# Four layers of a graph network on one core: where the mixing's weighing products stand, and how many passes stand between the steps of its chunks

## The chip, the cores and the metric

The kernel runs on one core of one Trainium2 chip. The time is device microseconds of one execution; before the change it is 1750.03 us, the median of three runs (1749.34 to 1750.75).

## What is computed

Four graph layers run one after the other over x (8 batches, 2048 nodes, 64 features) and a dense adjacency matrix of 2048 x 2048. Each ends as `x = layernorm(x + layer(x))`. The change lies in layers 0 and 1:

```
# layer 0, its end: industry = (adj / deg) @ (x @ W_ind), g = sum over hyperedges
pair = stack([industry, g])
s = tanh(pair @ fcW + fcb) @ av          # two scores per node
out = softmax(s over the two) weighs industry and g
x = layernorm(x + out)
# layer 1
deg = sum(adj + I); dinv = deg ** -0.5
x = layernorm(x + (dinv * (adj + I) * dinv) @ x @ W.T)
# layer 2 begins with softmax(relu(E @ E.T)) of the node embeddings E
```

A softmax over two scores is a sigmoid of their difference, so the kernel forms `g - 1`, `industry` and weighs their difference by `0.5 * (1 + tanh(0.5 * (s1 - s2)))`.

## The kernel before

**Tiling.** Two batches make a pair of 128 features; there are four pairs (NP = 4). The 2048 nodes are 16 tiles of 128 (t) or 4 chunks of 512 (c, NCH = 4). The transposed adjacency stays in SBUF. A product with it is made of **passes**: one pass is one matmul of 128x512 (line 172, the helper `mm`), with a 128x128 block of the left operand as weights and a 512 column piece of the adjacency. The left operand is split into a high and a low part (`v0h`, `v0l` to `v3h`, `v3l`, one pair of tiles for each chunk of nodes), so a pair needs 2 column groups x 16 tiles x 2 parts x 2 columns = 128 passes.

**The filler.** The passes do not stand in loops of their own. Generators yield after each pass, and `fill(n)` (line 420) draws n of them between other work, so that PE has passes to do while DVE, ACT and POOL work at the rest. `products` (line 342) gives layer 0's adjacency products and the degrees, 576 passes in all; `layer1` (line 1012) follows with 128 passes for each pair. When the part that a pass of layer 1 needs has not been made yet, `layer1` yields `"wait"`: that fill issues nothing and only counts a tick. Each pass counts a tick too (`tick`, line 321), and `after(n, f)` and `later(n, f)` run f so many ticks later. That is how work on DVE, ACT and POOL is put in its place; most of it is pinned in the written order (`pin`, line 838), and each engine takes its instructions in the order in which they stand.

**The mixing (end of layer 0).** 16 steps (4 pairs x 4 chunks). For chunk i:

- `mix_load` (line 871) fetches the stored product u0 and the inverse degrees; `mix_ind` (879) makes industry from it: products `pi`, then a multiplication on DVE (885). `mix_g` (887) fetches g (`gn`), transposes it on PE (`pg`) and copies it with -1 on ACT (899).
- `mix_scores` (906): four products `pf` (two batches of industry, two of g), each with a tanh on ACT (916); 5 ticks later the two differences on DVE (921); at once industry minus g on POOL (923); 8 ticks later `r + gn` on POOL (926).
- `mix_weigh` (928): two products `pd` of the differences with av, tanh on ACT (`th`, 935), and 4 ticks later the weighed difference on DVE (937).
- `mix_end` (940): transposes of it (`pt`), then, by ticks, the addition to r (957), the layer norm (853 to 865: sums on DVE, square on ACT, power on POOL, scaling on DVE) and `end` (947): r is stored to HBM (948), the load of x for chunk i + 2 is issued (305), and `l1_parts` is called for it where it is due.

The products of all these (`pi`, `pg`, `pf`, `pd`, `pt`, and layer 1's `po`) rotate through four PSUM banks (tag "mm").

**The hand-over to layer 1.** `l1_parts(p, c)` (line 963) loads the stored chunk again (`y`, 969), scales it by dinv on POOL 16 ticks later (972), and 6 ticks after that splits it: the high part on ACT (167), the low part on DVE (168). Passes of pair p then read it: chunk q of the pair's nodes is first read 16 q passes into its 128. `l1_end` (984) closes a column group with eight matmul instructions `po`, a row sum on DVE and POOL (991, 992) and a layer norm.

**E.** When all 16 chunks are stored, the pools of the mixing are closed, the memory is given to `xn`, and the embeddings are loaded into a part of it (1098). `make_el` (1105) splits them chunk by chunk and makes the bias product `pb`; `load_xn` (1005) fetches the first three pairs' results once `room` is set. What is left of the filler follows, and then layer 2's `apt_tile` (1144) and products `ua`.

DMAs are issued in order from SP's queue (loads and stores of the mixing), from ACT's (`load_xn`) and from POOL's.

Of the kernel before, what the change touches and what calls it, by code (L numbers as in the profile page):

```python
# [56 lines left out]
def tile_gnn_fast(  # L57
# [32 lines left out]
    NCH = N // C  # L90
# [8 lines left out]
    def cols(c, n=C):  # L99
        return slice(c * n, (c + 1) * n)  # L100
# [70 lines left out]
    def mm(*args, **kw):  # L171
        tc.keep_in_program_order(nc.tensor.matmul(*args, **kw))  # L172

    def transpose(dst, src):
        tc.keep_in_program_order(nc.tensor.transpose(dst, src, ident))  # L175
# [141 lines left out]
    def after(n, f, *more):  # L317

        soon.append([n, lambda: (f(), after(*more) if more else None)])

    def tick():
        for e in pending + soon:
            e[0] -= 1
        while pending and pending[0][0] <= 0:
            pending.pop(0)[1]()
        for e in [e for e in soon if e[0] <= 0]:
            soon.remove(e)
            e[1]()
# [91 lines left out]
    def fill(n):  # L420
        for _ in range(n):
            if next(filler, None) == "wait":
                tick()

    def first_parts(c, where):
        where.add(c)
        if c in mixed and c in free:
            l1_parts(0, c)
# [402 lines left out]
    def wide(c):  # L831
        return slice(c * JT, (c + 1) * JT)
# [7 lines left out]
    def normalized(pool, r, dst, centred, then):  # L840

        groups = 2 * JT
        r, dst = grouped(r), grouped(dst)
        wide_r = [P, groups, F]
        var, vare, rstd, mean = (
            pool.tile([P, groups], F32, tag=f"ln_{n}", name=f"ln_{n}", bufs=2) for n in "verm"
        )
        xc = pool.tile(wide_r, F32, tag="ln_c", name="ln_c", bufs=1)
        squares, src = (xc, r) if centred else (r, xc)

        def square():
            if not centred:
                pin(nc.vector.tensor_reduce(mean, r, AX.X, ALU.add))
                pin(nc.vector.scalar_tensor_tensor(
                    xc, mean[:, :, None].to_broadcast(wide_r), -1.0 / F, r, op0=ALU.mult, op1=ALU.add
                ))
            pin(nc.scalar.activation(squares, src, AF.Square))

        def power():
            pin(nc.vector.tensor_reduce(var, squares, AX.X, ALU.add))  # L860
            pin(nc.vector.tensor_scalar(vare, var, 1.0 / F, EPS, op0=ALU.mult, op1=ALU.add))
            pin(nc.gpsimd.tensor_tensor(rstd, vare, neg_half[:, :groups], ALU.pow))

        def scale():
            pin(nc.vector.tensor_tensor(dst, src, rstd[:, :, None].to_broadcast(wide_r), ALU.mult))
            then()

        return square, 5, power, 9, scale
    steps = NP * NCH

    def mix_load(i):
        if i < steps:
            p, c = divmod(i, NCH)
            uts[i] = mp0.tile([P, C], F32, tag="ut0", name="ut0", bufs=2)
            nc.sync.dma_start(uts[i], u0_hbm[p][:, cols(c)])
            invs[i] = mp0.tile([P, C], F32, tag="inv0", name="inv0", bufs=2)
            nc.sync.dma_start(invs[i], inv_hbm[:, cols(c)])

    def mix_ind(i):

        pi = lps.tile([P, C], F32, tag="mm", name="pi", bufs=4)
        mm(pi, lhsT=bd_ind, rhs=uts.pop(i), start=True, stop=True)
        inds[i] = mp.tile([P, C], F32, tag="ind", name="ind", bufs=3)
        inv = invs.pop(i)
        after(3, lambda: pin(nc.vector.tensor_tensor(inds[i], pi, inv, ALU.mult)))

    def mix_g(i):

        p, c = divmod(i, NCH)
        gn = mp.tile([P, JT, P], F32, tag="gn", name="gn", bufs=2)  # L890
        nc.sync.dma_start(
            gn, gs_hbm.rearrange("(p t) f -> p t f", t=NT)[:, wide(c), p * P:(p + 1) * P]
        )
        gns[i] = gn
        pg = lps.tile([P, C], F32, tag="mm", name="pg", bufs=4)
        for j in range(JT):
            transpose(pg[:, cols(j, P)], gn[:, j, :])
        gts[i] = mp.tile([P, C], F32, tag="gt", name="gt", bufs=2)
        pin(nc.scalar.activation(gts[i], pg, AF.Identity, bias=-1.0))

    def mix_x(i):
        if i < steps:
            rs[i] = mp.tile([P, JT, P], F32, tag="r", name="r", bufs=2)
            load_x(rs[i], *divmod(i, NCH))

    def mix_scores(i):

        t1 = []
        for src in (inds[i], gts[i]):
            for b in range(2):  # L910

                s = slice(b * F, (b + 1) * F)
                pf = lps.tile([P, C], F32, tag="mm", name="pf", bufs=4)
                mm(pf, lhsT=fc2[s, :], rhs=src[s, :], start=True, stop=True)
                t1.append(mp.tile([P, C], F32, tag="t1", name="t1", bufs=4))
                pin(nc.scalar.activation(t1[-1], pf, AF.Tanh, bias=fcb_col))
        tts[i] = t1[0:2]

        def differences():
            for b in range(2):  # L920
                pin(nc.vector.tensor_tensor(t1[b], t1[b], t1[2 + b], ALU.subtract))

        pin(nc.gpsimd.tensor_tensor(inds[i], inds[i], gts[i], ALU.subtract))
        after(5, differences)
        r, gn = rs[i], gns.pop(i)
        after(8, lambda: pin(nc.gpsimd.tensor_tensor(r, r, gn, ALU.add)))

    def mix_weigh(i):

        pd = lps.tile([P, C], F32, tag="mm", name="pd", bufs=4)  # L930
        for b in range(2):

            mm(pd[b * F:(b + 1) * F, :], lhsT=av2, rhs=tts[i][b], start=True, stop=True)
        th = mp.tile([P, C], F32, tag="th", name="th", bufs=1)
        pin(nc.scalar.activation(th, pd, AF.Tanh, scale=0.5))
        after(4, lambda: pin(
            nc.vector.scalar_tensor_tensor(inds[i], th, 1.0, inds[i], op0=ALU.add, op1=ALU.mult)
        ))

    def mix_end(i):  # L940
        p, c = divmod(i, NCH)
        r = rs.pop(i)
        pt = lps.tile([P, C], F32, tag="mm", name="pt", bufs=4)
        for j in range(JT):
            transpose(pt[:, cols(j, P)], inds[i][:, cols(j, P)])

        def end():
            nc.sync.dma_start(x1_hbm[p][:, wide(c), :], r)
            mix_x(i + 2)
            stored.add((p, c))  # L950
            if p == 0:
                first_parts(c, mixed)
            elif (p, c) in due:
                l1_parts(p, c)

        def add_up():
            pin(nc.vector.scalar_tensor_tensor(
                r, pt.rearrange("p (t f) -> p t f", f=P), 0.5, r, op0=ALU.mult, op1=ALU.add
            ))

        after(3, add_up, 0, *normalized(mp, r, r, False, end))

    def l1_parts(p, c):

        if (p, c) not in stored:
            due.add((p, c))
            return
        y = staged("y")
        nc.sync.dma_start(y, x1_hbm[p][:, wide(c), :])

        def scale():
            pin(nc.gpsimd.tensor_tensor(y, y, dinv[:, wide(c), None].to_broadcast([P, JT, P]), ALU.mult))

        def cast():
            part[p, c] = split(va, y, f"v{c}", 1, [P, JT, P], pin=True)

        after(16, scale, 6, cast)
# [27 lines left out]
    def load_xn():  # L1005

        for p in range(NP - 1):
            if room and done[p] == NCH:
                done[p] = 0
                nc.scalar.dma_start(xn[p], x2_hbm[p][:])  # L1010
# [42 lines left out]
    mix_x(1)  # L1053
    fill(4)
    for i in range(steps + 1):
        k = 9 if i > NCH else 8
        if i < steps:
            mix_scores(i)
            fill(k)
        if i > 0:  # L1060
            mix_end(i - 1)
            fill(k)
        if i + 1 < steps:
            mix_load(i + 2)
            mix_ind(i + 1)
            mix_g(i + 1)
            fill(k)
        if i < steps:
            mix_weigh(i)
            fill(k)  # L1070
    while len(stored) < steps:
        fill(1)
# [43 lines left out]
        nc.scalar.copy(bias, pb)  # L1116
        nc.sync.dma_start(bias_hbm[:, wide(c), :], bias)

    fill(32)
    for c in range(NCH):  # L1120
        make_el(c)
        fill(16)
        if c == 1:

            room.append(True)
            load_xn()
# [474 lines left out]
    for u in range(2, UNITS):  # L1601
        c, k = divmod(u, 2)
# [1002 lines left out]
```

## Time and profile before

| what | value |
| --- | --- |
| median of three runs | 1750.03 us (1749.34 to 1750.75) |
| the profiled execution | 1747.23 us |
| its span, first to last instruction | 1745.0 us |
| granted PE clock, mean | 0.981 |
| PE busy | 1662.8 us, 95% of the span |
| DVE / ACT / POOL busy | 48% / 34% / 33% |
| mixing, its first scores to its last transposes | 241.5 to 463 us |
| E, its first bias product | 484.12 us |
| first product of layer 2 (`ua`) | 517.01 us |

All times of the trace are microseconds from the start of the span, and one execution was profiled. A row of the timeline has the start, the duration, the engine, the line of the code, the operation, the tile written and those read, the size, and how often; what stands in brackets is idle time of that engine ahead of it and what ended it. Matmuls overlap, so the time that one costs is read from the starts of those that follow, not from its duration. A matmul of f32 operands is two instructions in the trace.

### The profile page before, as it was taken

What the parts mean: (1) busy time and instruction counts of PE and PEld (TensorE: products, weight loads), DVE (VectorE), ACT (ScalarE), POOL (GpSimd) and SP (SyncE); (2) the same over time, 40 slices, a digit from 0 to 9 for tenths busy, and PEclk for the clock granted to TensorE, in tenths of its full rate; (3) what the DMA queues carried; (4) which work ended last, traced back from release to release, by engine and by line L of the source; (5) the groups of instructions that cost most, each with busy time, mean ns of one, the idle gap of its engine ahead of it and who ended that gap; (6) DMA issues with size and microseconds to landing.
All of it is one profiled execution on the core that took longest, in us unless ns stands there. A gap on an engine that the chain in (4) does not pass through costs nothing. (4 is left out here: it accounts for less than half of the span.)

```text
span 1745.0 us, 27987 instructions
## 1 busy us (share of the span) xinstructions
PE 1662.8 (95%) x11196; PEld 1214.8 (70%) x11196; DVE 832.9 (48%) x1547; ACT 588.9 (34%) x1031; POOL 573.6 (33%) x515
## 2 busy tenths in 40 slices
PE   6888899999989999999999989999989999999996
PEld 4666666666664444468788878888768877878775
DVE  7679945678642221210137147777623433433332
ACT  1345533434321212112213257878512222222221
POOL 4578845556534443422023001222310200202001
PEclk9899999999999999999999989999989999999998
DMA  9743344444340000017344547585571121211111
GB/s 334 253 158 124 103 131 140 151 140 145 97 141 6 30 19 12 24 66 292 111 140 130 137 105 157 133 171 131 150 273 43 49 61 43 61 47 42 57 43 39
DMA packets 171180, 195.83 MB, mean 112 GB/s; under 512 B 71536, under 2 KB 116336, under 8 KB 169760
## 3 DMA queue, kind: packets, MB, share of 16 engines
q1 hardware_dynamic: 160096, 154.54, 30.0%
q0 software_dynamic: 8544, 30.68, 5.3%
q10 hardware_dynamic: 2400, 8.72, 1.4%
q8 instruction: 90, 1.47, 0.4%
q14 instruction: 50, 0.41, 0.1%
HBM read 126.72 MB, written 67.17 MB: 111 GB/s over the span
## 5 line engine op out<-in xcount | busy, mean ns | idle before, releaser
L172 PE MATMUL ua<-pt,xn 128*128 128x512 f32 x512 | 230.2, 592 | 1.4 <-DVE pt L1150 1.4
L172 PEld LDWEIGHTS ua<-pt,xn 128*128 128x128 f32 x512 | 96.9, 190 | 111.1 <-issue 104.0
L1502 DVE COPY w_half<-pw 128x512 f32<-128x512 f32 x160 | 109.7, 705 | 91.2 <-PE pw L172 90.6
L1498 ACT COPY w_half<-pw 128x1024 f32<-128x1024 f32 x128 | 129.8, 1014 | 51.4 <-PE pw L172 51.4
L172 PE MATMUL py<-w_half,xg 128*32 128x128 f32 x4096 | 142.6, 280 | 1.2 <-issue 1.2
L172 PE MATMUL u<-adj,v0h 128*128 128x512 f32 x384 | 134.0, 426 | 1.1 <-ACT h L1800 1.1
L172 PE MATMUL u<-adj_more,v2h 128*128 128x512 f32 x384 | 126.5, 408 | 0.0
L172 PEld LDWEIGHTS py<-w_half,xg 128*32 128x32 f32 x4096 | 111.6, 138 | 18.9 <-issue 2.1
L172 PE MATMUL u<-adj,v0l 128*128 128x512 f32 x384 | 124.6, 402 | 0.0
L172 PE MATMUL u<-adj_more,v2l 128*128 128x512 f32 x384 | 124.2, 400 | 0.0
L172 PE MATMUL pw<-est,wst 64*128 64x256 f32 x1024 | 111.2, 322 | 4.9 <-ACT w_half L1498 2.7
L1156 POOL TENSOR_TENSOR acc<-acc,pt 128x512 f32<-128x512 f32 x60 | 76.5, 1274 | 104.3 <-DVE pt L1150 103.6
L172 PEld LDWEIGHTS pw<-est,wst 64*128 64x128 f32 x1024 | 84.5, 189 | 27.6 <-ACT w_half L1498 20.0
L1150 DVE TENSOR_SCALAR pt<-pt 128x512 f32<-128x512 f32 x64 | 29.6, 462 | 153.0 <-ACT pt L1149 152.8
L1709 ACT CAST ar<-fcav 128x512 fp32r<-128x512 f32 x64 | 39.5, 618 | 166.8 <-DMA fcav<-in_adj_t 165.9
L172 PE MATMUL u<-adj_more,v3l 128*128 128x512 f32 x288 | 94.2, 403 | 0.0
L172 PE MATMUL u<-adj,v1h 128*128 128x512 f32 x288 | 93.7, 403 | 0.0
L1149 ACT ACTIVATE pt<-s 128x512 f32<-128x512 f32 x64 | 38.0, 598 | 164.8 <-PE s L172 164.8
L172 PE MATMUL u<-adj_more,v3h 128*128 128x512 f32 x288 | 93.6, 403 | 0.0
L1710 DVE SCALAR_TENSOR_TENSOR ar<-fcav,ar 128x512 f32<-128x512 f32 x64 | 44.7, 698 | 100.9 <-ACT ar L1709 100.9
L172 PE MATMUL u<-adj,v1l 128*128 128x512 f32 x288 | 92.0, 397 | 0.0
L1681 POOL TENSOR_TENSOR x<-x,rows 128x512 f32<-128x512 f32 x16 | 22.7, 1439 | 210.8 <-PE pt L175 129.3
(406 smaller groups left out, 3282.6 us busy)
## 6 DMA issues: line engine op xcount, KB each, us to landing
fcav<-in_adj_t SPq DMA_DIRECT2D x64, 256.0 KB, 2.9
u_hbm<-ut SPq DMA_DIRECT2D x48, 256.0 KB, 2.8
xg<-u_hbm SPq DMA_DIRECT2D x24, 512.0 KB, 8.5
adj<-in_adj_t POOLq DMA_DIRECT2D x16, 512.0 KB, 7.7
adj_more<-in_adj_t POOLq DMA_DIRECT2D x16, 512.0 KB, 7.7
adj_hbm<-adj_more SPq DMA_DIRECT2D x16, 512.0 KB, 5.5
x_hbm<-r SPq DMA_DIRECT2D x28, 256.0 KB, 2.7
hs_hbm<-st ACTq DMA_DIRECT2D x8, 584.0 KB
```

What stands on the lines that cost most here:

```text
L172: tc.keep_in_program_order(nc.tensor.matmul(*args, **kw))
L1149: nc.scalar.activation(pt, s, AF.Exp)
L1150: nc.vector.tensor_scalar(pt, pt, 1.0, None, op0=ALU.max)
L1156: nc.gpsimd.tensor_tensor(accs[c], accs[c], pt, ALU.add)
L1498: pin(nc.scalar.copy(dst, pw.rearrange("p j o n -> p n (j o)")))
L1502: pin(copy(dst[:, :, 2 * j:2 * j + 2], bank.rearrange("p o n -> p n o")))
L1681: nc.gpsimd.tensor_tensor(xs, xs, b2.to_broadcast([P, JT, P]), ALU.add)
L1709: nc.scalar.copy(ar, seen_a)
L1710: nc.vector.scalar_tensor_tensor(ar.bitcast(F32), seen_a, 1.0, ar.bitcast(F32), op0=ALU.mult, op1=ALU.not_equal, accum_out=left[:, t, k:k ...
```

## The change

In `mix_scores` the addition `r + gn` is taken out and becomes a function of its own, `mix_sum`, called behind the loads of the next chunk. In the loop of the steps `mix_weigh(i - 1)` now stands directly ahead of `mix_scores(i)`; before, it was the last thing in its own step, with passes behind it. `mix_end(i - 1)` moves from behind the scores to the end of step i. A step has three gaps of 11 passes (12 from step 5 on) in place of four of 8 (9). In the last round, which has no scores, 24 passes stand between the weighing and the transposes. Ahead of E `fill(56)` replaces `fill(32)`, between E's chunks `fill(12)` replaces `fill(16)`, and `room` is set behind E's first chunk in place of its second.

```diff
@@ mix_scores
         pin(nc.gpsimd.tensor_tensor(inds[i], inds[i], gts[i], ALU.subtract))
         after(5, differences)
+
+    def mix_sum(i):
         r, gn = rs[i], gns.pop(i)
         after(8, lambda: pin(nc.gpsimd.tensor_tensor(r, r, gn, ALU.add)))
@@ the steps
     for i in range(steps + 1):
-        k = 9 if i > NCH else 8
+        k = 12 if i > NCH else 11
+        if i > 0:
+            mix_weigh(i - 1)
         if i < steps:
             mix_scores(i)
-            fill(k)
-        if i > 0:
-            mix_end(i - 1)
             fill(k)
         if i + 1 < steps:
             mix_load(i + 2)
             mix_ind(i + 1)
             mix_g(i + 1)
+        if i < steps:
+            mix_sum(i)
             fill(k)
-        if i < steps:
-            mix_weigh(i)
+        if i == steps:
+            fill(2 * k)
+        if i > 0:
+            mix_end(i - 1)
             fill(k)
@@ E
-    fill(32)
+    fill(56)
     for c in range(NCH):
         make_el(c)
-        fill(16)
-        if c == 1:
+        fill(12)
+        if c == 0:
             room.append(True)
             load_xn()
```

## The prediction, on record before the changed kernel ran

> **What bounds the kernel now.** I read the forty slices first: they tell which engine is never idle, and where even that one is.
>
> ```profile
> PE   6888899999989999999999989999989999999996
> PEclk9899999999999999999999989999989999999998
> ```
>
> TensorE (PE) is at nine tenths nearly everywhere. Of the stretch that the change touches (slices 6 to 12, 230 to 515 us) slice 11 alone is at 8, with a lower clock beside it. Then busy time by stretch (PE, weight loads, DVE, ACT, POOL, PE clock, DMA share, GB/s):
>
> ```profile
> 250.00:300.00 50.00, 50.00 (x218) 31.63 (x216) 27.99 (x39) 19.83 (x34) 23.59 (x22) 1.00 0.38 127
> 400.00:458.00 58.00, 58.00 (x264) 37.93 (x263) 44.38 (x64) 23.17 (x41) 37.74 (x26) 1.00 0.36 124
> 458.00:490.00 32.00, 23.98 (x95) 19.31 (x94) 20.80 (x36) 8.01 (x15) 15.05 (x11) 0.79 0.53 170
> ```
>
> Inside the mixing PE has no idle time to win. The loss sits in 32 us at its end. PE's timeline there:
>
> ```profile
> 455.37 0.63 PE L172 MATMUL u<-adj_more,v2l 128*128 128x512 f32 x2
> 455.93 1.08 PE L172 MATMUL pd<-t,fcav 128*64 128x512 f32 x4
> 456.94 0.73 PE L172 MATMUL u<-adj_more,v2h 128*128 128x512 f32 x2
> ...
> 458.91 0.40 PE L172 MATMUL u<-adj_more,v3h 128*128 128x512 f32 x1
> 462.91 1.11 PE L175 MATMUL pt<-ident,ind 128*128 128x128 f32 x4 [3.60 <-DVE ind L937]
> ...
> 479.30 0.40 PE L172 MATMUL u<-adj_more,v2l 128*128 128x512 f32 x1
> 484.12 1.93 PE L172 MATMUL pb<-bp,xn 16*128 16x64 f32 x8 [4.42 <-issue]
> ```
>
> The reader is to see two holes: the last chunk's transposes (pt) wait for its weighed difference, and E's first product (pb) waits, as the ACT row at 483.94 shows, for the embedding that the DMA brings. Behind each, for about 5 us, a pair of passes takes 0.85 us instead of 0.467 (starts 464.25, 465.10, 465.95).
>
> Last, what chunk 15 has to do between its pt and the first pass that needs it (v3h and v3l of pair 3), from the timeline of all engines:
>
> ```profile
> 465.84 0.68 DVE L957 SCALAR_TENSOR_TENSOR r<-pt,r 128x512 f32<-128x512 f32 x1
> 470.93 1.64 POOL L862 TENSOR_TENSOR ln_r<-ln_e,neg_half 128x8 f32<-128x8 f32 x1 [5.56 <-DVE ln_e L861]
> 474.14 0.32 SPq L948 DMA_DIRECT2D x_hbm<-r  x1
> 476.95 0.32 SPq L969 DMA_DIRECT2D y<-x_hbm  x1
> 479.91 1.09 POOL L972 TENSOR_TENSOR y<-y,dinv 128x512 f32<-128x512 f32 x1 [0.84 <-DMA y<-x_hbm]
> 481.03 0.62 ACT L167 CAST v3h<-y 128x512 fp32r<-128x512 f32 x1 [1.29 <-POOL y L972]
> 481.69 0.69 DVE L168 TENSOR_TENSOR v3l<-y,v3h 128x512 fp32r<-128x512 f32 x1 [1.58 <-ACT v3h L167]
> ```
>
> From pt (462.91) to v3h (481.65) are 18.7 us, 7.5 of them behind the store. Now they hide behind passes that need other chunks.
>
> **Passes as a clock.** I number the 1088 passes: 576 of the products, then 128 for each pair. 406 precede the first scores in both programs. A pass costs 0.2335 us (pairs start 0.467 apart). Pair 3 reads chunk 2's part from pass 992 and chunk 3's from 1008; pair 2 reads its chunk 3 from 880. Counting the fills: before, 24 in step 0, 32 in steps 1 to 4, 36 in 5 to 14, so chunk 15's scores stand at 918, its weighing at 936, its pt at 945. After, 22, then 33, then 36: weighing at 956, pt at 980. So pt and pass 1008 are 28 passes apart, where they were 63. In the changed program twelve of the 56 fills ahead of E find no part and issue nothing. This is the change's price.
>
> **What goes.** (a) The wait ahead of the last pt: from 458.91 to 469.10 stand 14 passes and one pt. At full speed: 14 x 0.2335 + 0.45 (pt with the slower pass behind it) = 3.7; it took 10.2. Gone: 6.5, of it 3.8 idle and 2.7 slow clock. 24 passes (5.6 us) now cover a wait of 3.8. (b) The wait ahead of pb: from 479.30 to 489.65 stand 10 passes and a pb (1.2): 3.55 of 10.35. Gone: 6.8, since 34 passes now stand between chunk 15's first use and E. (c) At the start the second pg waited 0.68 for its load (L891); it comes three passes later: 0.7. (d) Weighing and scores change the product's shape: pairs 0.467 apart become 0.56 ahead of pd and 0.57 behind it, about 0.09 and 0.10, and as much around pf. Standing together they have one return to passes less. The step from pd to pf is not in the trace; it costs between nothing and as much as both. So 0 to 0.19 in each of 15 steps; I take half, 1.5.
>
> The Trainium skill ("TensorEngine Tiling (Array Packing)", Key Properties) says that a change of tiling mode, not of tile alone, drains the engine. By it the step from pd (128x64) to pf (64x128) is such a change, one of four goes, and the sum gets 1.5 of the 2.9; no row here shows that step alone. Sum of what goes: 15.5.
>
> **What comes.** (e) Chunk 15 at pass 1008. PE arrives 0.45 + 28 x 0.2335 = 7.0 after pt's start. How late is the part? Least: chunk 13 ran undisturbed,
>
> ```profile
> 438.70 0.69 DVE L957 SCALAR_TENSOR_TENSOR r<-pt,r 128x512 f32<-128x512 f32 x1 [0.43 <-PE pt L175]
> ...
> 444.19 0.69 DVE L865 TENSOR_TENSOR r<-ln_c,ln_r 128x512 f32<-128x512 f32 x1
> ```
>
> with pt at 438.07, so 6.8 to the end of its normalization; plus 7.5 from store to v3h: 14.3. Chunk 15's own in the trace: 18.7. Most: in the changed order DVE has the low part of chunk 14 (v2l, L168) directly behind chunk 15's add, ahead of its mean. That part waits for its own y, whose buffer a pair-2 row sum (L992) frees; and POOL has two other powers (1.65 each) ahead of chunk 15's. Taking chunk 14's pt 11.9 earlier (36 passes, a pd 1.2, two po of 0.9, a pt), with the rows above I get up to 22. I take 19.5, near the row and above it for these queues: 12.5 idle. A stall this long is followed by the slow clock; both holes above lost 2.2 to 2.7 there, I take 2.4. Together 14.9 (9.7 to 17.4). Any wait of PE at 992 for chunk 14 lies inside, since chunk 15's chain does not wait for PE.
>
> (f) Chunk 11 at pass 880. Before, pt at 408.71, v3h at 427.32 (18.6 later), first used at 433.39: 6.1 to spare. After, the two are 44 passes apart instead of 61, with a pt, two po, a pd and pf (3.2), a pi with pg (1.3) and a pt between: 10.3 + 7.2 = 17.5. So 1.1 late with the same chain. Longer: the next scores now follow within 12 passes, their differences (L921) precede chunk 11's last scaling on DVE, and two of the four "mm" banks that pf rotates through belong to po just issued: up to 5. Shorter: none. I take 3.0 (0 to 5, and 2.4 more if PE cools). The trace has waits of 1.73 and 1.43 with no slow pairs behind them and of 3.60 with; 3 lies between.
>
> The Trainium skill ("TensorE: Matmul & The Clock Gate", What's actually happening) puts the limit at an idle window of about 3.4 us; by it a wait of 3.0 cools nothing, and the sum stands without those 2.4.
>
> **Costed at nothing.** mix_sum's add moves behind the next chunk's loads in POOL's and SP's order: gn's buffer comes free a step (15.2 us from pt to pt) before its transposes, its load lands in 2.9; if not, PE waits as at the start, 1.7. In the moved weighing the fourth pf takes pd's bank and waits for th (0.60 on ACT), behind three pf of 0.48; without that cover 0.6 a step. The x2 loads (L1010) are opened at E's first chunk: some 80 passes, 18 us, cover them; uncovered, the first ua would wait. No passes are left behind E's last chunk, where 29 were: the squares of the embedding now stand behind four pt on DVE, and four rounds of ua (3.67 us each) cover their load (3.7) and 1.2 of work.
>
> **Sum.** -15.5 + 14.9 + 3.0 = +2.4 us. The profiled execution took 1747.23 (span 1745.0 and 2.2 around it) and would take 1749.6; the runs shown have a median of 1750.03, so I state 1752.4.
>
> **Rivals.** 1: the parts come early. If the queues do not hold chunk 15 up, (e) is 9.7 and (f) 1.1: -4.7, 1745.3, faster. For it: chunk 13 did run so; against: v2l stands in its way. With (f) at 3.0 it decides at 17.1 us from pt to v3h. 2: chunk 11 comes in time: -0.6, 1749.4. For it: 6.1 to spare now; against: 17 passes fewer. 3: both come late and PE cools twice: 17.4 + 7.4 - 15.5 = +9.3, 1759.3. For it: queues in order, where one late load delays the next chunk; against: pair 1's last part is 60 passes from its pt (692 to 752), so nothing is late to begin with. That the change only moves the hole from pt and pb to the parts is the forecast itself.
>
> **Chances.** Forecast 0.46, rival 1 0.24, rival 2 0.14, rival 3 0.16. A measurement of this kernel tells about 0.2%, 3.5 us. The forecast, 2.4, is close to that line: 0.24 same, 0.22 slower. Rival 1: 0.22 faster, 0.02 same; rival 2: 0.02 faster, 0.10 same, 0.02 slower; rival 3: slower. Faster 0.24, same 0.36, slower 0.40. The extremes, -7.2 (all low ends) and +10.8, each need every bound at once; 1744 to 1759 leaves out the outer fifth.
>
> **What would show it.** Ahead of the last pt and of pb no wait; one hole of 10 to 14 us at the first v3h behind them, released by ACT v3h, with slow pairs behind; some 3 us at pair 2's v3h. Wrong if v3h comes under 17 us from pt, if PE waits inside the steps (pf on th or po), or if pg waits for gn in many steps.

## The result, and the profile after

The changed kernel takes 1767.57 us in the median of five runs (1763.14 to 1772.47), the kernel before 1750.72 in five runs beside it (1749.34 to 1751.01). The ratio is 1.0104, 95% interval 1.0091 to 1.0116: the change makes the kernel 1.0% slower, and the time lies above the predicted range. The profiled execution took 1763.14 us, with a span of 1761.3.

The forty slices, to be laid beside those of before:

```profile
PE   6888899989969999999999999999989999999996
PEclk9899999999989999999999989999999999999998
```

The twelfth digit, the 8 of before (480 to 523 us), has become a 6 (484 to 528), its clock has an 8 that the row of before does not show, and the ninth digit (352 to 396 us) has gone from 9 to 8. So the loss lies in the stretch that the prediction looked at, but not in one place of it only. From the first `pg` (238.45 us) to the first `ua` (536.26) the changed kernel takes 297.8 us, the kernel before 277.0 (240.01 to 517.01). These 20.8 us are more than the difference of the two spans, 16.3: outside of this stretch the profiled execution of the changed kernel happened to be 4.5 us quicker.

PE's waits between 235 and 545 us of the changed kernel (total, times, longest):

```profile
PE u L172 <- ACT v3h L167: 11.5, 1, 11.5
PE pf L172 <- ACT th L937: 4.9, 3, 3.9
...
PE pf L172 <- DVE r L993: 3.3, 2, 2.4
PE po L172 <- ACT ut L1037: 2.7, 3, 1.0
```

The first row was forecast. The waits of `pf` were not: they lie inside the steps, between the weighing and the scores that now stand behind it, and the prediction had named just these as what would show it wrong. (In the changed kernel and those made from it the lines from 926 on stand two or more later: `th` is line 937, the row sum of `po` 993. Kernels made from the one before keep its lines.) The wait of `pb`, and that of the last `pt`, are gone.

**The forecast hole.** Chunk 15 in the timeline of all engines, from its transposes to the pass that needs it:

```profile
485.35 0.60 PE L175 MATMUL pt<-ident,ind 128*128 128x128 f32 x4
487.46 0.68 DVE L959 SCALAR_TENSOR_TENSOR r<-pt,r 128x512 f32<-128x512 f32 x1
491.58 0.67 DVE L853 TENSOR_REDUCE ln_m<-r 128x8 f32<-128x512 f32 x1
498.00 0.32 SPq L950 DMA_DIRECT2D x_hbm<-r  x1
...
506.12 0.62 ACT L167 CAST v3h<-y 128x512 fp32r<-128x512 f32 x1 [12.40 <-POOL y L974]
506.79 1.22 PE L172 MATMUL u<-adj_more,v3h 128*128 128x512 f32 x2 [11.55 <-ACT v3h L167]
```

`pt` no longer waits, but from `pt` to the first pass with v3h are 21.4 us, and PE has only 28 passes to put there.

**The hole that was not forecast.** PE, POOL and ACT around the scores at 374 us:

```profile
372.08 1.28 POOL L928 TENSOR_TENSOR r<-r,gn 128x512 f32<-128x512 f32 x1 [1.46 <-DMA r<-in_x_n]
372.98 1.08 PE L172 MATMUL pd<-t,fcav 128*64 128x512 f32 x4
...
374.94 1.04 POOL L974 TENSOR_TENSOR y<-y,dinv 128x512 f32<-128x512 f32 x1
374.95 1.02 PE L172 MATMUL pf<-gt,fcav 64*128 64x512 f32 x2
376.01 0.62 ACT L167 CAST v3h<-y 128x512 fp32r<-128x512 f32 x1 [4.73 <-POOL y L974]
...
379.25 0.58 ACT L937 ACTIVATE th<-pd 128x512 f32<-128x512 f32 x1
379.88 1.23 PE L172 MATMUL pf<-gt,fcav 64*128 64x512 f32 x2 [3.91 <-ACT th L937]
```

Read it from the bottom. The fourth `pf` takes `pd`'s PSUM bank and so waits for `th`, the tanh that reads `pd`. `th` itself needs 0.58 us and could have run at 374; but ACT takes its instructions in order, and ahead of `th` stands the split of (pair 1, chunk 3), which waited 4.73 us for POOL's `y`, and behind that a square (378.71 us), whose input on DVE in turn stood behind the split's low part. POOL was busy with `r + gn`, which the change has moved behind the next chunk's loads, and which had waited for its x, and with a power between the two. Undisturbed, the stretch from `pd` to the next `pi` takes 5.8 us (`pd` 1.01, the four `pf` 0.96 and 0.95, six pairs of passes and 0.10); here it takes 12.4 (372.98 to 385.35), so 6.5 are lost, with slow pairs behind the wait.

The second such place has another queue, DVE's:

```profile
427.92 0.69 DVE L168 TENSOR_TENSOR v2l<-y,v2h 128x512 fp32r<-128x512 f32 x1 [5.67 <-ACT v2h L167]
429.85 0.68 DVE L993 TENSOR_TENSOR r<-po,dinv 128x512 f32<-128x512 f32 x1
430.59 1.12 PE L172 MATMUL pf<-ind,fcav 64*128 64x512 f32 x2 [2.42 <-DVE r L993]
...
432.55 2.60 PE L172 MATMUL pf<-gt,fcav 64*128 64x512 f32 x4 [0.84 <-DVE r L993]
```

Two banks that `pf` needs belong to layer 1's `po`; their row sums stand on DVE behind a low part that waits for its split. The same stretch (426.05 to 439.66) takes 13.6 us, 7.8 too many.

### The profile page after: what moved, and what is told of

Read it like the earlier page. It is cut to its first block, busy times and chain, and to the rows that moved or that the text cites. A ratio compares the mean times of both kernels' runs of the same rounds, so it can differ in the third digit from the quotient of the medians.

```text
span 1761.3 us, 27982 instructions
## 1 busy us (share of the span) xinstructions
PE 1663.1 (94%) x11196; PEld 1214.2 (69%) x11196; DVE 829.1 (47%) x1547; ACT 589.4 (33%) x1031; POOL 575.5 (33%) x515
```

## The experiments

Two readings were to be told apart. **Theory:** the hole for chunk 15 costs some 10 us and comes from the passes at the end, and the rest comes from in-order queues that now stand between a score product and its bank. **Rival:** the new order, with weighing and scores side by side, costs by itself. Ratios are to the kernel before, run on the same chip; its medians there were 1750.7 us for the changed kernel and 1747.3 to 1748.3 for the others.

| kernel | median, us | ratio (95% interval) |
| --- | --- | --- |
| changed | 1767.57 | 1.0104 (1.0091 to 1.0116) |
| before + E's part | 1748.95 | 1.0008 (0.9996 to 1.0021) |
| changed order alone | 1756.82 | 1.0044 (1.0029 to 1.0059) |
| changed, two splits later | 1759.29 | 1.0063 (1.0041 to 1.0085) |
| changed, sum later still | 1784.33 | 1.0211 (1.0185 to 1.0237) |
| changed, 9 passes for 24 | 1758.32 | 1.0052 (1.0035 to 1.0069) |
| changed order, two splits later | 1749.09 | 1.0011 (0.9994 to 1.0027) |
| before, one split later | 1744.85 | 0.9985 (0.9973 to 0.9997) |
| before + E's part, x2 loads on SP | 1741.78 | 0.9960 (0.9946 to 0.9974) |
| before, both of these | 1739.16 | 0.9947 (0.9930 to 0.9964) |
| changed order, chunk's end earlier | 1749.13 | 1.0004 (0.9992 to 1.0017) |
| changed, three buffers for gn | 1768.62 | 1.0116 (1.0095 to 1.0137) |
| changed, one split a tick later | 1769.05 | 1.0126 (1.0109 to 1.0143) |

**E's part alone, on the kernel before.**

```diff
-    fill(32)
+    fill(56)
     for c in range(NCH):
         make_el(c)
-        fill(16)
-        if c == 1:
+        fill(12)
+        if c == 0:
```

> The kernel before with only E's part of the change: 56 passes ahead of E, 12 between its chunks, room at the first. Theory (the loss of the change comes from the order of the steps and from the last round, not from E): the wait of 4.4 us ahead of pb goes with its slow pairs, 6.8 us: 1744, and no new wait. Rival A (the passes ahead of E are what hurts, since 12 of the 56 are void in the changed kernel and none is left behind E): 1755 or more.

Neither theory's number came: no gain, 1.0008. In the kernel before `pb` waited for the embedding, which reached ACT only then:

```profile
483.94 0.62 ACT L1107 CAST el<-xn 128x512 fp32r<-128x512 f32 x1 [2.29 <-DMA xn<-in_emb]
```

That wait is gone, as the theory had it, but a new one has come. ACT (its queue, then its engine) and PE:

```profile
493.82 0.33 ACTq L1010 DMA_DIRECT2D xn<-x_hbm  x1
494.19 0.37 ACT L1116 COPY bias<-pb 128x256 f32<-128x256 f32 x1 [4.83 <-DMA x_hbm<-r]
494.46 0.59 ACT L1035 COPY ut<-u 128x512 f32<-128x512 f32 x1
495.10 1.67 PE L172 MATMUL po<-bd_w,ut 128*128 128x128 f32 x8 [3.22 <-ACT ut L1035]
```

The third load of x2 is issued from ACT's queue and waits there for pair 2's store. Behind it stands the copy `ut`, and PE's `po` waits for that. PE got there sooner, and found another late thing.

**The new order alone**: the changed kernel with 9 passes for 24 behind the last weighing, and E's old numbers.

```diff
-            fill(2 * k)
+            fill(9)
...
-    fill(56)
+    fill(32)
...
-        fill(12)
-        if c == 0:
+        fill(16)
+        if c == 1:
```

> The changed kernel with the old fills at the end: 9 passes in place of 24 behind the last weighing, 32 and 16 at E, room at E's second chunk; the new order of the steps stays. Theory (chunk 15's chain from its weighing to v3h sets the end of pair 3's first group, and the holes at pf in the steps come from the order): the holes at pf stay, chunk 15 comes up to 4 us earlier: 1763 to 1766. Rival A (the passes at the end cost most of it): 1755 or less.

1.0044, so between the two, and both had the shares wrong: the passes at the end cost more than half, 0.6 of the 1.04%. The hole for chunk 15 is gone altogether. Chunk 15's part is ready at 498.3, 16.9 us after its `pt`, just ahead of PE, which comes to pass 1008 at 498.49. The waits of `pf` for `th` (4.4 us) and for the row sum (2.9) remain.

**Two splits behind `th`**, in the changed kernel: those of (pair 1, chunk 3) and (pair 2, chunk 2) run 11 ticks later, so that on ACT they stand behind `th` and on DVE behind the row sums.

```diff
-        after(16, scale, 6, cast)
+        after(16, scale, 17 if (p, c) in ((1, 3), (2, 2)) else 6, cast)
```

> The changed kernel with the split of two parts, (pair 1, chunk 3) and (pair 2, chunk 2), put 11 ticks later, behind th on ACT and behind the row sums of po on DVE. Theory (the fourth pf takes pd's PSUM bank and waits for th, which stands on ACT behind the high part of a chunk that is late; likewise the third pf behind po's row sum, which stands on DVE behind the low part): both holes at pf (3.9 and 3.3 us of idle time, with slow pairs 6.5 and 7.8 us in all) go, and some 3 to 5 come back at pair 2's v3h: 1756 to 1759. Rival B (POOL waits in the moved sum for the load of r, and what stands behind it, the scaling of the part and the power, is late whatever the order on ACT): less than 2 us gained, 1766 or more.

1.0063: 1759.29 us, 0.3 above the theory's 1756 to 1759, and far from the rival's 1766. Nothing about banks, products or passes was changed, and both unforeseen holes are gone (`pf` for `th` 2.1 us in two waits, none for the row sum). And what they had hidden appears, a wait of 4.10 us for pair 2's v3h at 441.02 us.

**The sum still later**: `after(8, ...)` of `mix_sum` becomes `after(22, ...)`, to take `r + gn` out of the way of `y` on POOL.

> The changed kernel with the moved sum r + gn 14 ticks later, so that POOL scales the parts and takes the powers ahead of it. Rival B (the moved sum's wait on POOL is the root): both holes at pf go and chunk 15 comes earlier: 1755 or less. Theory: the parts come 1 to 3 us earlier, which shortens the first hole and leaves the second: 1762 to 1766.

Both missed, 1.0211. PE's largest wait:

```profile
PE pg L175 <- DMA gn<-gs_hbm: 21.0, 11, 4.3
```

`r + gn` is the last to read gn's buffer. Later, it frees the buffer later, the load of the next g comes late in 11 steps, and `pg` waits. The prediction had put gn's release at nothing for the change's own delay, and that held (3.3 us in three waits, 2.4 in two before); a further 14 ticks cost 17.7 us more of it. Of the rival's mechanism one half did come: `pf` waits only 1.5 us for `th` and 0.8 for the row sum in this run. But `pg`'s waits have shifted every chain against the others, so the run does not tell whether the moved sum on POOL or the order on ACT and DVE is the root of the two holes; what is shown is that reordering ACT and DVE ends them.

**9 passes for 24, E as changed.** The edit is the first of the two above.

> The changed kernel with 9 passes in place of 24 between the last weighing and the last transposes; E keeps its new fills (56, 12, room at its first chunk). Theory, that the hole at pass 1008 comes from those 15 passes alone: in the run with both parts taken back that hole was gone and the kernel 10 us faster, so here too the wait for v3h of pair 3 is under 3 us and the time is 1752 to 1759 us. Rival, that E's early opening makes chunk 15 late (its y was 4.9 us from issue to POOL beside the embedding's and x2's loads, 2.8 where those came later): the wait stays at 7 us or more and the time at 1762 us or more.

1.0052, so the theory held (the profiled execution, 1762.74 us, was the slowest of ten); the passes alone bring the changed kernel down by half of its loss, and with the run of the order alone at 1.0044, E's new numbers show no effect of their own here. DVE and PE, for chunk 15:

```profile
484.60 1.11 PE L175 MATMUL pt<-ident,ind 128*128 128x128 f32 x4 [2.42 <-DVE ind L939]
486.89 0.69 DVE L959 SCALAR_TENSOR_TENSOR r<-pt,r 128x512 f32<-128x512 f32 x1
...
489.02 0.68 DVE L993 TENSOR_TENSOR r<-po,dinv 128x512 f32<-128x512 f32 x1
...
501.56 0.73 PE L172 MATMUL u<-adj_more,v3h 128*128 128x512 f32 x2 [1.23 <-ACT v3h L167]
```

15 passes are 3.5 us, but the wait falls by 10.3. PE arrives later (from `pt` to pass 1008 are 43 passes, a wait for v2h and two `po`), and the part comes sooner: from `pt` to v3h are 17.0 us where the changed kernel had 21.4. Of these 4.4 us 3.6 lie between `pt` and the store, where chunk 15's add and mean now stand ahead of pair 2's row sums (489.02) and not behind them; the rest lies behind the store.

**Order alone and the two splits later**: both edits together.

> The new order of the steps with the old numbers of passes at the end (9 behind the last weighing; E 32, 16, room at its second chunk), and the splitting of two parts, (pair 1, chunk 3) and (pair 2, chunk 2), 11 ticks later, so that it stands behind th and the row sum instead of ahead of them. Theory, that what the order costs is two queues, ACT's ahead of th and DVE's ahead of the row sum: the waits of pf at 378 and 430 us go, 4 to 5 us each with the slow passes behind them, and 1756.8 becomes 1747 to 1750 us. Rival, that weighing and scores side by side cost by themselves (banks, changes of shape): waits inside the steps stay and the time is 1753 us or more.

1.0011, the theory's number. The rival falls here: weighing and scores stand side by side, and the kernel is as fast as the one before. Of the waits of `pf` one of 0.8 us is left. What the order still loses is chunk 11's part, at pass 880: PE waits 4.67 us for pair 2's v3h at 439.13 us. Beside it stand a wait of 2.95 for the last weighed difference (3.60 in the kernel before) and 3.2 of `pg` for gn in three waits (2.4 in two before). A gain from the order itself does not show.

**The same cause in the kernel before**: there the last transposes waited for a weighed difference, and `th` of chunk 15 stood behind the split of (pair 3, chunk 0):

```profile
460.11 0.62 ACT L167 CAST v0h<-y 128x512 fp32r<-128x512 f32 x1 [1.97 <-POOL y L972]
460.64 0.59 ACT L935 ACTIVATE th<-pd 128x512 f32<-128x512 f32 x1
462.17 0.68 DVE L937 SCALAR_TENSOR_TENSOR ind<-th,ind 128x512 f32<-128x512 f32 x1
```

The edit:

```diff
-        after(16, scale, 6, cast)
+        after(16, scale, 17 if (p, c) == (3, 0) else 6, cast)
```

> The kernel before, with one split moved: (pair 3, chunk 0) 11 ticks later. In the order of the engines that swaps v0h and th on ACT, and v0l and the weighed difference on DVE, and nothing else. Theory, that a split queued ahead of th is what makes the last transposes wait (3.6 us idle, 2.7 us of slow passes): they start about 2.2 us earlier, the wait falls under 1.6 us and the slow passes go, 1747.3 becomes 1742 to 1744 us. Rival, that the weighed difference is late for its own chain (scores, differences, th): the wait stays above 3 us and the time within 1.5 us of the kernel before.

0.9985, a gain of 3 us (the theory had 3.3 to 5.3), and the mechanism as drawn, with the wait of the last `pt` at 1.72 us (the theory had under 1.6):

```profile
455.79 0.58 ACT L935 ACTIVATE th<-pd 128x512 f32<-128x512 f32 x1
457.86 0.62 ACT L167 CAST v0h<-y 128x512 fp32r<-128x512 f32 x1 [1.49 <-POOL y L972]
458.50 0.66 PE L175 MATMUL pt<-ident,ind 128*128 128x128 f32 x4 [1.72 <-DVE ind L937]
```

Part of the gain is given back at once: PE is earlier at E, and `pb` waits 5.5 us where it waited 4.4.

**E's part with the x2 loads on SP's queue**, on the kernel before: `nc.scalar.dma_start(xn[p], ...)` becomes `nc.sync.dma_start(xn[p], ...)`, beside E's edit above.

> The kernel before with E's part of the change (56, 12, room at its first chunk), and the three loads of x2 issued from SP's queue instead of ACT's. In the run with E's part alone the wait ahead of pb was gone, but ACT's third x2 load waited for its store until 493.82 us, with the copy ut behind it that PE's po needs (3.2 us idle and slow passes). Theory, that this load in ACT's queue ate E's gain: the wait of po on ut goes and the time is 1740 to 1743 us. Rival, that E's passes are only moved and something else is late (x2 itself, for the first ua): 1747 us or more, with a new wait behind E.

0.9960, as the theory had it. `ut` is copied at 489.09, the third load waits on SP until 492.53 and holds up nothing that PE needs soon. So E's new numbers are worth 6 of the 6.8 us that the prediction had for them, but only with the load out of ACT's queue. The loads on SP with E's old numbers were not run; in this stretch of the kernel before the profile lists no wait of PE for `ut`, so it shows nothing there for them to end.

**Both together.**

> The kernel before with the two edits that each helped it: the split of (pair 3, chunk 0) behind th (3.1 us gained alone) and E's new fills with the x2 loads on SP's queue (6.2 us gained alone). Theory, that they end two different waits: the gains add up, 1737 to 1740 us, with no wait of pb, and the last transposes waiting under 2 us. Rival, that PE only runs sooner into the next late thing (the embedding for pb, ut for po): a new wait takes a third or more of it, 1741 us or more.

0.9947: the gains add up, 8.5 us below the kernel before in the medians and, by the two ratios, 1.6% below the changed one. `pb` does not wait, and no new wait is over 1.2 us. What is left of waits in the stretch are 3.3 us of `pg` for gn in two, and single ones of 1.5 (`ua`), 1.5 (the last `pt`), 1.2 (`po` for `ut`) and 0.8 (`pf` for `th`).

**The new order with the chunk's end one gap earlier**: `mix_end(i - 1)` ahead of the next chunk's loads, 9 passes behind the last weighing, the splits of (1, 1), (2, 0) and (3, 1) behind `th`, and E's part with the loads on SP.

> The changed order, weighing directly ahead of the next scores, but with the transposes and the end of the chunk one gap earlier, ahead of the next chunk's loads; 9 passes behind the last weighing; the splits of (1, 1), (2, 0) and (3, 1) behind th; x2 loads on SP's queue; E 56, 12. Theory, that the change lost only where chunks end late and where a split is queued ahead of th, and that side by side the two products save some 0.19 us a step: no wait for v3h of pair 2 or pair 3, none of pf over 1 us, 1736 to 1742 us. Rival, that the order costs by itself (th between pd and the fourth pf, gn held longer): waits of pf and pg of 6 us or more together, 1746 us or more.

1.0004: the theory's number missed, and the rival's mechanism with it. Inside the steps no wait of `pf` or `pg` is over 1 us (0.8 and 0.3), and pair 2's v3h is in time. But chunk 15's chain has grown to 22.2 us (468.72 to 490.89), and pass 1008 waits again, 8.1 us. And the transposes, a gap nearer to their weighing, wait 5.7 us in three places. The parts of pair 2 come in time, and what that gains is given back at the end of the stage. The edit moves four things at once, so which of them lengthens the last chain is not shown.

**Three buffers for gn**, in the changed kernel (`bufs=3`).

> The changed kernel with three buffers for gn in place of two. Theory, that the late sum holds gn's buffer and so delays the next load, as the run with a still later sum showed on a larger scale: the waits of pg for gn (3.3 us in 3) go, and the kernel is 2 to 4 us faster than the changed one, so 0.7 to 0.95% slower than the kernel before. Rival, that the load is late for its place in SP's queue: the waits stay, and so does the time (1.0%).

Missed: the waits for gn fall from 3.3 to 1.8 us, the time does not (1.0116). `pf` waits 5.5 us for `th` and `po` 2.9 for `ut` there, 4.9 and 2.7 without the third buffer. The waits for gn are not what the change lost by.

**The split of (pair 3, chunk 2) one tick later**, in the changed kernel, so that chunk 15's mean is ahead of it on DVE (6 becomes 7 for that part).

> The changed kernel with the split of (pair 3, chunk 2) one tick later: on DVE its low part then stands behind chunk 15's mean and difference instead of ahead of them, on ACT its high part behind chunk 15's square; nothing else moves. Theory, that this low part, which waits for its own chain until 490.6 us, held chunk 15's mean from 488.2 to 491.6 us: v3h is ready 2 to 3.3 us earlier after pt than the 21.4 us of the changed kernel, PE waits up to 1.9 us longer for v2h and as much or more less for v3h (8 to 10 us), and the time falls by 1 to 3 us (ratio 1.0085 to 1.0105). Rival, that the DMAs and POOL's powers set chunk 15's end: from pt to v3h it stays over 20.5 us, and the time is that of the changed kernel or above.

The rival's: 1.0126, and 23.1 us from `pt` (487.03) to v3h.

```profile
489.85 0.69 DVE L853 TENSOR_REDUCE ln_m<-r 128x8 f32<-128x512 f32 x1
...
493.53 0.63 ACT L857 ACTIVATE ln_c<-r 128x512 f32<-128x512 f32 x1 [5.51 <-POOL r L994]
...
500.85 0.32 SPq L950 DMA_DIRECT2D x_hbm<-r  x1
510.18 1.22 PE L172 MATMUL u<-adj_more,v3h 128*128 128x512 f32 x2 [8.71 <-ACT v3h L167]
```

The mean is earlier (2.8 us behind `pt`, 6.2 before), but its square (ACT, 494.07 us) stands behind that of a row of pair 2, which waits for POOL. Freed in one queue, chunk 15 is held in the next.

## Why the prediction was wrong, point by point

- **The step that failed** stands under "Costed at nothing": "In the moved weighing the fourth pf takes pd's bank and waits for th (0.60 on ACT), behind three pf of 0.48; without that cover 0.6 a step." The bank and the wait were named, the price was that of `th` alone. What stands ahead of `th` on ACT was not asked, and there stands a split that waits for POOL and a load; at the second place it is the row sum of `po` on DVE that stands behind such a split's low part. The two places cost 6.5 and 7.8 us, together 14.3, where the sum had nothing. Putting two splits behind brings the changed kernel from 1.0104 to 1.0063, and the order alone from 1.0044 to 1.0011: by the ratios 6 to 7 us, and not 14, in part because a wait of 4 us returns at pair 2's v3h. Rival 3 held the slow case to be late parts alone.
- **(f), chunk 11 at pass 880**, predicted 3.0 (0 to 5) with `po`'s banks among its reasons. In the changed kernel PE never waits there, because the holes at 379 and 430 held PE back; with them gone the wait is 4.1 and 4.7 us, inside the bounds. The size was right. Of the reasons, `po`'s banks showed at another place: they stopped the scores themselves. The others were not tested one by one.
- **(e), chunk 15 at pass 1008**, predicted 14.9 (9.7 to 17.4). From `pt` to PE's first v3h are 21.4 us against 7.0 of passes, so 14.4 lost, of it 11.55 as one wait and 2.6 ahead of v2h and v2l, which the prediction had set inside; slow passes cost 1.8 more: 16.2. Right in size, with the chain at the long end of the 14.3 to 22, and in part by luck: one reason given for it, the low part ahead of chunk 15's mean, does not hold it by itself; with that part moved away the mean came earlier and the chain still grew, to 23.1. The runs with shorter chains (16.9 and 17.0) have chunk 15 ahead of pair 2's rows in three queues; which of these decides was not isolated, and stays open.
- **(a) and (b)**, 6.5 and 6.8 us gone: both waits are gone. That passes can buy this back is shown for (b) by E's part with the loads on SP (6 us); for (a) the smaller cure, one split later, gave 3.
- **(c)** did not come: the second `pg` waits 1.25 us where it waited 0.68, and in all `pg` waits 3.3 us in three waits, 2.4 in two before.
- **(d), the change of shape**, 0 to 0.19 in a step, half taken (1.5 us). From `pt` to `pt` the early steps take 12.58 us with 33 passes, 12.535 with 32 before: without the passes (0.2335 each) 4.87 and 5.06. So 0.19, the whole of it; if the later steps gain as much, 2.8 us in 15. The step from `pd` to `pf` starts 1.01 us behind `pd`, exactly as a pass does behind `pd` in the kernel before, and the `pf` behind it take 0.96 and 0.95, as they did: there is no gap at all. The Trainium skill ("TensorEngine Tiling (Array Packing)", Key Properties) has every change of tiling mode drain the engine; between these two shapes the trace shows none, while between either and the full 128x128 it shows 0.09 to 0.10.
- **Sum.** Gone 16.1 (6.5, 6.8, 2.8); come 16.2, 6.5 and 7.8, and some 5 in small waits (`po` on `ut` 2.7, `pf` on `th` 1.0, `gn` 1.2). That is 19 of the 20.8 us that the stretch has grown. The balance of the named terms was right to some 2 us (16.2 less 16.1, and nothing for (f), against a forecast of +2.4); the direction was forecast, and the term that was not in the sum made the size.
- **One row was misread**, without effect on the sum: the prediction has slice 11, counted from 0, at 8 "with a lower clock beside it", but the clock row of before has a 9 in that slice. The lower clock stands in the row of 458 to 490 us, 0.79.

## What to carry to other kernels

When a product is moved so that the next one takes its PSUM bank, the price is not the time of the instruction that reads the bank, but the wait of whatever stands ahead of that instruction in its engine's queue: list that queue, with each entry's own wait, at every place where the move happens. The same holds for a DMA issued from a computing engine's queue: it waits there for its source, and with it every copy behind it (4.83 us on ACT here). And where several chains end close together, passes shifted into one hole come out of the cover of another: here the gain came when a waiting instruction was taken out of the way of one that PE needed, and the moved passes paid only together with that.

## What the runs showed of the hardware

The length of a wait of PE does not by itself tell whether the slow clock follows. Behind waits of 2.61, 2.81 and 2.95 us pairs of passes start 0.85 us apart for a while, at once or up to 1.5 us behind the wait; behind one of 2.42 a `po` takes 1.56 us up to the next start in place of 0.81. Waits of no more than 1.97 (the changed kernel with two splits later, 322.36 us) and 2.00 (9 passes for 24, 247.79 us) were followed by a granted clock of 0.60 and 0.61 over the next 4 us. But behind waits of 1.72 and 2.24 all stays at full speed, and so it does behind one of 3.12 (sum later still, 398.90 us), with a granted clock of 1.00. A second short wait close behind does not settle it either: 2.29 with 0.45 (order alone) and 1.72 with 0.40 (three buffers for gn) are followed by slow pairs, 1.83 with 0.40 (changed) is not. What decides is not shown here.

The Trainium skill ("TensorE: Matmul & The Clock Gate", What's actually happening) speaks of an idle window of about 3.4 us, free-running; these runs show the slow clock behind waits up to 1.4 us shorter than that (by the trace's ends of matmuls, which are modelled). So the prediction's 3.0 us for (f) could have gone either way.
